# Making the one-hots, the shifted numbers and the transposed mask of a graph network on GpSimd, with a redrawn order of steps

## The chip, the core and the metric

The kernel runs on one core of a Trainium2 chip. A core has engines that work side by side, each through its own instructions in order: TensorE (PE; its weight loads are shown as PEld), VectorE (DVE), ScalarE (ACT), GpSimd (POOL) and SyncE (SP), which here issues nearly all the transfers between memories. They wait for each other through semaphores. Data stand in SBUF, on 128 partitions; TensorE writes its products to PSUM, which DVE and ACT can read and GpSimd can't. The metric is the time of one execution on the device, in microseconds (us).

## What is computed

A network of four layers over 128 graphs of 128 nodes with 64 features. Each layer normalises the features and adds its result to them. The first layer is the costly one, and the change lies in it:

```python
mask = (adj > 0.0).astype(x.dtype)
W1a, W1b = (W1[:F], W1[F:])
xj_proj = x @ W1a
diff = x[:, :, None, :] - x[:, None, :, :]
h = jax.nn.relu(xj_proj[:, :, None, :] + diff @ W1b + b1)
hm = jnp.einsum('bjkh,bjk->bjh', h, mask)
deg = jnp.sum(mask, axis=-1)
return hm @ W2 + deg[..., None] * b2
```

For every node j and every neighbour k of it (about an eighth of the nodes) a vector of H = 192 is formed, `relu(p[j] - q[k])`, and these are summed over the neighbours. Layer 1 is three matrix products with the adjacency and a head, layer 2 one product and a normalisation over the whole batch, layer 3 one product and a tanh.

## The kernel before

**Rounds.** The 128 graphs are worked on in 32 groups of G = 4. While one group is in the sum over neighbours, the next is sorted and projected, and the one before goes through layers 1 and 2. So in a steady state there is a round: the same mix of work on three neighbouring groups. Layer 3 follows at the end for all groups, after the sums over the batch.

**The sum over neighbours.** The kernel doesn't run over all 128 x 128 pairs. `sort` (line 535) numbers the neighbours of each node and sorts the nodes by how many they have. Step number n of a group then takes "the n-th neighbour of each node". A step has four parts, each a stream of its own:

- `pick` (709) makes the step's one-hot: a matrix with a 1 where the neighbour's number equals the wanted one. It is a comparison with a constant, from numbers in bf16 to 0 or 1 in bf16. Two sorts exist. `ohn` (128 x 1536, line 720) holds the one-hots of three steps at once, for near neighbours whose numbers come from `near_n`; there are NEAR = 4 in a group. `oh` (128 x 512, line 730) serves one step; there are FULL + BLOCKS = 5 + 3, five from `num` and three from `num_r`.
- `fill` (733) copies the sorted p, `psort` or `psort_r`, into one of three PSUM blocks `blk` (ACT).
- `subtract` (741) lets TensorE multiply the one-hot with q and add that into the block: q is gathered by a matrix product. A step with `oh` needs 12 products, as q is kept in three bf16 parts; a step with a third of `ohn` needs 4, from `near_q`.
- `gather` (756) takes the relu of the block and adds it to `acc` (DVE, `scalar_tensor_tensor` on 128 x 768).

A group has 20 steps. `ohn` has three buffers and `oh` five; `pick` may make the next one only when the step that used the buffer's last contents has been issued (lines 717 and 726).

**What stands around it.** In `sort`, ACT copies the transposed adjacency, `mT` (544) is its mask in bf16, TensorE counts with it (`ps_rankT`), DVE makes `leftT`, and so on to the sorting matrix `to_b`. GpSimd widens that to f32 (`to`, 593). The numbers `num` are copied out by ACT and sent through memory by SP (`n_dram`, then `near_n`, lines 609 to 611). `num_r` (627 to 636) are the numbers of the nodes with many neighbours, copied into segments and shifted by a constant for each segment: four `tensor_scalar` and one `tensor_tensor`. In `project` (639), GpSimd subtracts the third part of q (668), which SP then spreads into `near_q`, and adds the degree's share to x (675, 677). In `layer1` and `layer2_norm`, GpSimd makes four additions and products more. These eight instructions a round are GpSimd's whole work in the steady state.

**The order.** Within an engine the order of the program is the order of execution. It is made by `run_all` (1011): each stage of each group is a stream of steps, every step has a due time from a plan (`SORT_PLAN`, `PROJECT_PLAN`, ..., lines 49 to 55, with the groups PERIOD apart; `MOVED` and `OWN` for the first and last groups), and of the streams that may go on the one that is due first issues its next step. The plans are in units of 10 ns of a schedule that was worked out beforehand; on the chip they only set the order, the time comes from the engines and the waits.

All instructions are issued through one helper, so the profile puts them on its line 93; the tiles' names tell them apart.

Of the kernel before, what the change touches and what calls it, by code (L numbers as in the profile page):

```python
# [14 lines left out]
ALU = mybir.AluOpType  # L15
# [14 lines left out]
NEAR = 4  # L30
FULL = 5
BLOCKS = 3
SEGS = [76, 33, 11, 4, 2, 2]
STARTS = [sum(SEGS[:s]) for s in range(len(SEGS))]
# [10 lines left out]
MOVED = {('pick', -1): (49, 0.75), ('pick', -2): (-108, 1.095), ('fill', -1): (0, 0.75), ('fill', -2): (0, 1.0), ('subtract', -1): (-22, 0.752), ('subtract', -2): (21, 0.99), ('gather', -1): (0, 0.75), ('gather', -2): (20, 1.0), ('pick', 0): (-948, 0.849), ('fill', 0): (-93, 0.923), ('subtract', 0): (-63, 0.963), ('gather', 0): (-211, 0.71), ('sort', 0): (89, 0.76), ('sort', 1): (-572, 0.733), ('project', 0): (690, 0.648), ('project', 1): (-17, 1.008), ('after_layer0', 0): (0, 1.0)}  # L45
OWN = {('after_layer0', -2): [-663, 6, 139, 139, 387, 588, 694, 1072, 1098, 1186, 1287, 1312, 1312, 1472, 1598, 1676, 1789, 1789, 1972, 1972, 2122, 2482, 2482, 2482, 2482, 2717, 2869, 2913, 3118, 3160, 3171, 3319, 3423, 3497, 3650, 3650, 3804, 3804, 3839, 3858, 3896, 4188, 4290, 4321, 4633, 4697, 4724, 5099], ('first_half', -1): [-1189, -966, -886, -871, -753, -659, -570, -311, -230, -110, -107, -26, -26, 24, 49, 159, 231, 233, 351, 355, 454, 465, 465, 520, 582, 606, 717, 717, 879, 909, 909, 998, 1084, 1149, 1238, 1238, 1283, 1313, 1390, 1404, 1404, 1660, 1664, 1695, 1826, 1968, 1987, 2288], ('second_half', -1): [-1130, -987, -834, -770, -655, -586, -484, -231, -231, -153, -109, -52, -17, 45, 104, 176, 245, 247, 361, 365, 461, 472, 472, 525, 585, 608, 715, 745, 882, 913, 913, 1094, 1094, 1143, 1233, 1233, 1276, 1304, 1389, 1389, 1389, 1608, 1655, 1697, 1831, 1955, 1980, 2266], ('sort', 0): [-764, -520, -520, -118, 341, 397, 448, 545, 565, 586, 586, 586, 716, 719, 1143, 1143, 1539, 1889, 1889, 1889, 1889, 1889], ('project', 0): [-1552, -1066, -1066, -841, -472, 891, 1108, 2201, 3381, 3462, 3495, 3495, 3495, 3665, 3716, 3716, 3745, 3970, 3970, 3970, 3970, 4141, 4141, 4141, 4141, 4141, 4721, 5455, 5455]}
SET_UP_PLAN = [332, 1387, 1507, 1851, 1896, 1910, 1910, 2766]
PERIOD = 3491
SORT_PLAN = [-10, 215, 250, 378, 489, 489, 1032, 1058, 1156, 1168, 1185, 1185, 1446, 1511, 1511, 1575, 1776, 1776, 2087, 2287, 2309, 2309]
PROJECT_PLAN = [-2635, -2500, -1975, -1764, -1068, -475, 40, 1245, 1273, 1409, 1839, 1847, 1877, 2328, 2526, 2526, 2712, 2745, 2745, 2745, 2745, 2745, 2784, 3028, 3028, 3157, 3402, 3527, 3708]  # L50
PICK_PLAN = [-540, -447, -447, -276, -234, -22, 71, 77, 77, 77, 207, 1130, 1692, 2294]
FILL_PLAN = [-651, -523, -37, 207, 312, 687, 695, 888, 1110, 1226, 1432, 1432, 1606, 1644, 1929, 2176, 2386, 2562, 2724, 2886, 3026]
SUBTRACT_PLAN = [-1022, -1000, -991, -991, -991, -991, 205, 218, 476, 476, 699, 705, 715, 715, 715, 715, 936, 936, 936, 936, 984, 1048, 1230, 1504, 1504, 1511, 1760, 2121, 2121, 2305, 2305, 2419, 2419, 2783, 2851, 2851, 2902, 3090, 3152, 3168, 3252]
GATHER_PLAN = [-431, -241, 167, 444, 478, 731, 928, 1096, 1311, 1311, 1455, 1837, 2058, 2095, 2187, 2459, 2540, 2668, 2668, 2668, 3062]
AFTER_PLAN = [-636, -55, 123, 159, 454, 633, 843, 1365, 1400, 1517, 1608, 1727, 1799, 1930, 2098, 2203, 2347, 2353, 2590, 2597, 2796, 2819, 2819, 2929, 3055, 3102, 3327, 3385, 3651, 3713, 3728, 3925, 4064, 4163, 4337, 4337, 4423, 4476, 4618, 4644, 4655, 5082, 5218, 5260, 5500, 5761, 5797, 6329]
LATE = 14
WARM = 60
BEHIND = 3
# [50 lines left out]
def network(ctx, tc, io, out, over=None, x1=None):  # L109

    nc = Engines(tc)
# [42 lines left out]
    proj, near_q, near_n = [], [], []  # L154
# [175 lines left out]
    def set_up_first():  # L330

        yield
        nc.vector.tensor_scalar(wq, wp, -1.0, None, ALU.mult)
        nc.vector.tensor_tensor(wp, wp, wtop, ALU.add)
        done.add("w")
        yield
        centred(b2_all, F)
        yield from split_part(where["L0_gnn_b1"])
        for t in (near_q[1:] + near_n[1:]):
            nc.gpsimd.memset(t, 0.0)  # L340
        done.add("first")
        yield
# [76 lines left out]
    def flat(t):  # L419
        return t.rearrange("p a n -> p (a n)")  # L420
# [114 lines left out]
    def sort(g):  # L535
# [5 lines left out]
        adjT = adjTs[g]  # L541
        yield
        mT = once.tile([P, G, P], BF16, tag="mT", name="mT")
        nc.vector.tensor_scalar(mT, adjT, 0.0, None, ALU.is_gt)
        yield BANK
        pk = bank("ps_rankT")
        matmul(pk, upto_t, flat(mT), start=True, stop=True)
# [58 lines left out]
        num = edge.tile([P, G, P], BF16, tag="num", name="num")  # L606
# [19 lines left out]
        yield  # L626
        num_r = edge.tile([P, G, P], BF16, tag="num_r", name="num_r")
        for i in range(LIKE):
            nc.vector.tensor_scalar(num_r[:, :, STARTS[i] : STARTS[i] + SEGS[i]], num[:, :, 0 : SEGS[i]], float(-i * BLOCKS), None, ALU.add)
        m, n = len(SEGS) - LIKE, SEGS[LIKE]  # L630
        nc.vector.tensor_tensor(
            num_r[:, :, STARTS[LIKE] : P].rearrange("p b (m n) -> p b m n", n=n),
            num[:, :, 0:n].unsqueeze(2).to_broadcast([P, G, m, n]),
            behind.unsqueeze(1).unsqueeze(3).to_broadcast([P, G, m, n]),
# [74 lines left out]
    def pick(g):  # L709

        yield lambda: g in sorts
        for n, (third, i) in enumerate(ORDERS.get(g, ORDER)):
            t = g * per + n
            if third is not None:
                if (g, i) not in nears:
                    k = len(nears)
                    yield lambda: k < 3 or near_last[k - 3] in ready
                    near_last.append(max(g * per + m for m, kind in enumerate(ORDERS.get(g, ORDER)) if kind[0] is not None and kind[1] == i))
                    oh = nears[g, i] = ohn.tile([P, 3, G, P], BF16, tag="ohn", name="ohn")
                    nc.vector.tensor_scalar(oh.rearrange("p t b n -> p (t b n)"), near_n[g % 2].rearrange("p t b n -> p (t b n)"), float(i + 1), None, ALU.is_equal)  # L720
                    onehots[t] = oh[:, third]
                else:
                    onehots[t] = nears[g, i][:, third]
                continue
            k = len(other_last)
            yield lambda: k < 5 or other_last[k - 5] in ready
            other_last.append(t)
            num = sorts[g][0 if i < FULL else 1]
            oh = ohp.tile([P, G, P], BF16, tag="oh", name="oh")
            nc.vector.tensor_scalar(flat(oh), flat(num), float(NEAR + i + 1), None, ALU.is_equal)  # L730
            onehots[t] = oh

    def fill(g):
# [285 lines left out]
    if x1 is not None:  # L1019
        run(set_up_first())  # L1020
        run(set_up())
        for g in range(NG - 1):
            run(after_layer0(g))
    else:
        streams = []
        early = -9 * PERIOD
        streams.append(Stream(set_up_first(), SET_UP_PLAN, early))
        streams.append(Stream(set_up(), REST_PLAN, 0))
        for g in range(NG):
            for stage, plan, start in (  # L1030
                (sort, SORT_PLAN, (g - 1) * PERIOD if g else early),
                (project, PROJECT_PLAN, (g - 1) * PERIOD if g else early),
                (pick, PICK_PLAN, g * PERIOD),
                (fill, FILL_PLAN, g * PERIOD),
                (subtract, SUBTRACT_PLAN, g * PERIOD),
                (gather, GATHER_PLAN, g * PERIOD),
                *(((after_layer0, AFTER_PLAN, (g + 1) * PERIOD),) if g < NG - SPLIT else ((first_half, AFTER_PLAN, (g + 1) * PERIOD), (second_half, AFTER_PLAN, (g + 1) * PERIOD))),
            ):
                key = stage.__name__, g if g < 2 else g - NG
                later, scale = MOVED.get(key, (0, 1.0))  # L1040
                streams.append(Stream(stage(g), OWN.get(key, plan), start + later, scale))
        streams.append(Stream(squares(), SQUARES_PLAN, (NG - 1) * PERIOD))
        streams.append(Stream(filler(), FILLER_PLAN, (NG - 1) * PERIOD))
        run_all(streams)
# [319 lines left out]
```

## Time and profile before

| | us |
|---|---|
| runs of the kernel before: median (lowest to highest) | 1360.82 (1359.75 to 1364.78) |
| the profiled execution | 1361.02 |
| its span, first to last instruction | 1359.0 |
| mean clock granted to TensorE in it | 0.98 |
| busy: ACT | 974.6 (72%) |
| busy: GpSimd | 327.7 (24%), 408 instructions |
| first and last `oh` on DVE start at | 25.0 and 1183.7 |

After the last step of the last group there follow about 165 us of batch sums and layer 3.

How to read it: the profile lists for each engine when each instruction was at work. Its groups of instructions are written "engine operation out<-in shapes xcount | busy us, mean ns of one | idle time of the engine just before them, and what ended it". The chain of waits follows the work that ended last back from the end, at each step to what released it; "issue" is time in which the engine waited for nothing that shows. A line of busy time by engine has the stretch, its length, then PE, PEld, DVE, ACT and POOL, each with the number of instructions, the granted clock, the share of the transfer engines that was in use and GB/s.

GpSimd's larger instructions in the steady state, by their mean: the subtraction for q 1651 ns, the addition to the adjacency 1286, the widening of `to` 766, the others 615 to 761. In the 1359 us it stood idle for 308.7 us until ACT had made q, 291.2 us until DVE had made t, and 234.2 us until DVE had made `to_b`.

### The profile page before, as it was taken

What the parts mean: (1) busy time and instruction counts of PE and PEld (TensorE: products, weight loads), DVE (VectorE), ACT (ScalarE), POOL (GpSimd) and SP (SyncE); (2) the same over time, 40 slices, a digit from 0 to 9 for tenths busy, and PEclk for the clock granted to TensorE, in tenths of its full rate; (3) what the DMA queues carried; (4) which work ended last, traced back from release to release, by engine and by line L of the source; (5) the groups of instructions that cost most, each with busy time, mean ns of one, the idle gap of its engine ahead of it and who ended that gap; (6) DMA issues with size and microseconds to landing.
All of it is one profiled execution on the core that took longest, in us unless ns stands there. A gap on an engine that the chain in (4) does not pass through costs nothing.

```text
span 1359.0 us, 29824 instructions
## 1 busy us (share of the span) xinstructions
PE 1195.3 (88%) x11031; PEld 983.3 (72%) x11031; DVE 1138.3 (84%) x2573; ACT 974.6 (72%) x1871; POOL 327.7 (24%) x408
## 2 busy tenths in 40 slices
PE   5689999999999999998989999999999988889787
PEld 2467777777777777777777777777777777777566
DVE  6888988888888888888888888888888888735894
ACT  3577777777788777777777777777877777743653
POOL 3421122211221112221112221221211222012983
PEclk9899999999999999999999999999999999986899
DMA  2222222222222122222222222222222221100254
GB/s 81 78 70 68 67 70 61 68 73 72 72 73 73 53 70 65 67 67 67 70 66 65 68 69 73 72 72 72 63 62 64 65 63 58 40 9 9 78 153 116
DMA packets 106997, 92.41 MB, mean 68 GB/s; under 512 B 45135, under 2 KB 90460, under 8 KB 106844
## 3 DMA queue, kind: packets, MB, share of 16 engines
q1 hardware_dynamic: 106380, 90.17, 23.1%
q8 instruction: 89, 1.46, 0.5%
q14 instruction: 64, 0.52, 0.1%
q10 hardware_dynamic: 464, 0.26, 0.1%
HBM read 34.12 MB, written 16.71 MB: 37 GB/s over the span
## 4 chain that ended last, share of the span: by engine, by line
DVE 45%; PE 40%; issue 6%; POOL 3%; ACT 3%; SPq 1%; DVEq 1%; DMA 0%; ACTq 0%; POOLq 0%
DVE acc L93 24%; PE blk L93 17%; PE ps_pr L93 5%; PE ps_ag L93 4%; PE ps_sA L93 4%; PE ps_p L93 4%; DVE x L93 2%; PE ps_q L93 2%; DVE h L93 2%; PE ps_ga L93 2%; DVE lower L93 2%; SPq L93 1%; DVE rank L93 1%; DVE rank_t L93 1%; DVE to_b L93 1%
## 5 line engine op out<-in xcount | busy, mean ns | idle before, releaser
L93 DVE SCALAR_TENSOR_TENSOR acc<-blk,acc 128x768 f32<-128x768 f32 x576 | 545.3, 951 | 102.3 <-PE blk L93 68.7
L93 ACT COPY blk<-psort 128x768 f32<-128x768 f32 x544 | 428.2, 803 | 43.4 <-DVE acc L93 42.1
L93 PE MATMUL blk<-q,oh 128*128 128x192 bf16 x3072 | 302.5, 247 | 46.9 <-ACT blk L93 43.6
L93 PEld LDWEIGHTS <-oh 128*128 128x128 bf16 x3072 | 260.9, 99 | 81.2 <-issue 72.8
L93 PE MATMUL blk<-near_q,ohn 128*128 128x192 bf16 x1536 | 183.8, 246 | 18.6 <-ACT blk L93 16.1
L93 PEld LDWEIGHTS <-ohn 128*128 128x128 bf16 x1536 | 134.1, 99 | 61.5 <-issue 49.9
L93 POOL TENSOR_TENSOR q<-rest,q 128x768 bf16<-128x768 f32 x32 | 52.8, 1651 | 308.7 <-ACT q L93 308.6
L93 POOL TENSOR_TENSOR x<-x,t 128x260 f32<-128x260 f32 (+1 forms) x33 | 24.0, 729 | 291.2 <-DVE t L93 291.2
L93 ACT COPY blk<-psort_r 128x768 f32<-128x768 f32 x96 | 78.6, 818 | 16.3 <-DVE acc L93 16.0
L93 PEld LDWEIGHTS ps_pr<-g,dT 128*128 128x128 f32 x504 | 71.3, 192 | 20.4 <-issue 7.0
L93 POOL CAST to<-to_b 128x512 f32<-128x512 bf16 x32 | 24.5, 766 | 234.2 <-DVE to_b L93 234.2
L93 DVE TENSOR_SCALAR ohn<-near_n 128x1536 bf16<-128x1536 bf16 x128 | 80.5, 630 | 0.0
L93 PE MATMUL ps_pr<-g,dT 128*128 128x128 f32 x504 | 78.6, 279 | 0.6 <-ACT dT L93 0.5
L93 PE MATMUL ps_ag<-adjT,msg 128*128 128x128 f32 x504 | 68.8, 279 | 0.0
L93 ACT ACTIVATE dT<-ps_ag 128x512 f32<-128x512 f32 (+1 forms) x96 | 57.6, 600 | 7.1 <-PE ps_ag L93 4.9
L93 ACT ACTIVATE rstd<-var,eps 128x4 f32<-128x4 f32 (+1 forms) x98 | 29.4, 300 | 45.4 <-DVE var L93 45.4
L93 PEld LDWEIGHTS ps_ag<-adjT,msg 128*128 128x128 f32 x504 | 61.5, 192 | 0.2 <-ACT sB L93 0.2
L93 ACT COPY psort<-ps_p 128x384 f32<-128x384 f32 x64 | 30.7, 479 | 41.8 <-PE ps_p L93 41.8
L93 PE MATMUL ps_q<-wq,hT 128*128 128x384 f32 x128 | 59.1, 546 | 0.8 <-ACT hT L93 0.5
L93 PE MATMUL ps_sA<-fro,acc 128*128 128x128 f32 x248 | 50.2, 284 | 9.2 <-DVE acc L93 8.6
L93 ACT ACTIVATE sq<-x 128x256 f32<-128x256 f32 (+1 forms) x98 | 39.7, 407 | 19.4 <-DVE x L93 19.4
L93 PE MATMUL ps_p<-wp,hs 128*128 128x384 f32 x128 | 53.0, 496 | 0.6 <-ACT hs L93 0.5
(272 smaller groups left out, 2595.9 us busy)
## 6 DMA issues: line engine op xcount, KB each, us to landing
near_q<-q SPq DMA_DIRECT2D x288, 63.0 KB
near_n<-n_dram SPq DMA_DIRECT2D x96, 126.0 KB
a<-in_adj_dram SPq DMA_DIRECT2D x32, 256.0 KB
adjT_dram<-adjT SPq DMA_DIRECT2D x32, 256.0 KB
adjT<-adjT_dram SPq DMA_DIRECT2D x32, 256.0 KB
psort_r<-psort SPq DMA_DIRECT2D x32, 228.0 KB
fro_r<-fro SPq DMA_DIRECT2D x32, 152.0 KB
x<-in_x_dram SPq DMA_DIRECT2D x32, 128.0 KB
```

The costliest lines, as they stand in the source:

```text
L93: ins = op(*args, **kw)
```

## The change

The comparisons for `ohn` and `oh`, the transposed mask `mT` and the five instructions for `num_r` are issued on GpSimd instead of DVE. Their operands, buffers and gates stay. `PERIOD` and the seven plans of the steady state are new numbers; `MOVED`, `OWN`, the set-up plans and the plans of the end are unchanged. Of the plans, those for projecting and picking are shown; sorting, filling, subtracting, gathering and the layers after are redrawn in the same manner.

```diff
-PERIOD = 3491
+PERIOD = 3436
...
-PROJECT_PLAN = [-2635, -2500, -1975, -1764, -1068, -475, 40, 1245, 1273, 1409, 1839, 1847, 1877, 2328, 2526, 2526, 2712, 2745, 2745, 2745, 2745, 2745, 2784, 3028, 3028, 3157, 3402, 3527, 3708]
-PICK_PLAN = [-540, -447, -447, -276, -234, -22, 71, 77, 77, 77, 207, 1130, 1692, 2294]
...
+PROJECT_PLAN = [-3200, -3200, -3200, -3200, -3200, -3185, -760, 1256, 1345, 1387, 1651, 1745, 1821, 2240, 2315, 2369, 2429, 2706, 2706, 2706, 2706, 2706, 2726, 2849, 2865, 3006, 3033, 3096, 3274]
+PICK_PLAN = [-1036, -1030, -995, -995, -995, -995, -660, -575, 579, 642, 700, 1003, 1228, 1228]
...
         mT = once.tile([P, G, P], BF16, tag="mT", name="mT")
-        nc.vector.tensor_scalar(mT, adjT, 0.0, None, ALU.is_gt)
+        nc.gpsimd.tensor_scalar(mT, adjT, 0.0, None, ALU.is_gt)
...
         for i in range(LIKE):
-            nc.vector.tensor_scalar(num_r[:, :, STARTS[i] : STARTS[i] + SEGS[i]], num[:, :, 0 : SEGS[i]], float(-i * BLOCKS), None, ALU.add)
+            nc.gpsimd.tensor_scalar(num_r[:, :, STARTS[i] : STARTS[i] + SEGS[i]], num[:, :, 0 : SEGS[i]], float(-i * BLOCKS), None, ALU.add)
         m, n = len(SEGS) - LIKE, SEGS[LIKE]
-        nc.vector.tensor_tensor(
+        nc.gpsimd.tensor_tensor(
...
-                    nc.vector.tensor_scalar(oh.rearrange("p t b n -> p (t b n)"), near_n[g % 2].rearrange("p t b n -> p (t b n)"), float(i + 1), None, ALU.is_equal)
+                    nc.gpsimd.tensor_scalar(oh.rearrange("p t b n -> p (t b n)"), near_n[g % 2].rearrange("p t b n -> p (t b n)"), float(i + 1), None, ALU.is_equal)
...
-            nc.vector.tensor_scalar(flat(oh), flat(num), float(NEAR + i + 1), None, ALU.is_equal)
+            nc.gpsimd.tensor_scalar(flat(oh), flat(num), float(NEAR + i + 1), None, ALU.is_equal)
```

More of the change, by code (lines that the diff above doesn't have):

```diff
@@ L47 @@
 SET_UP_PLAN = [332, 1387, 1507, 1851, 1896, 1910, 1910, 2766]
-PERIOD = 3491
-SORT_PLAN = [-10, 215, 250, 378, 489, 489, 1032, 1058, 1156, 1168, 1185, 1185, 1446, 1511, 1511, 1575, 1776, 1776, 2087, 2287, 2309, 2309]
-PROJECT_PLAN = [-2635, -2500, -1975, -1764, -1068, -475, 40, 1245, 1273, 1409, 1839, 1847, 1877, 2328, 2526, 2526, 2712, 2745, 2745, 2745, 2745, 2745, 2784, 3028, 3028, 3157, 3402, 3527, 3708]
-PICK_PLAN = [-540, -447, -447, -276, -234, -22, 71, 77, 77, 77, 207, 1130, 1692, 2294]
@@ L52 @@
-FILL_PLAN = [-651, -523, -37, 207, 312, 687, 695, 888, 1110, 1226, 1432, 1432, 1606, 1644, 1929, 2176, 2386, 2562, 2724, 2886, 3026]
-SUBTRACT_PLAN = [-1022, -1000, -991, -991, -991, -991, 205, 218, 476, 476, 699, 705, 715, 715, 715, 715, 936, 936, 936, 936, 984, 1048, 1230, 1504, 1504, 1511, 1760, 2121, 2121, 2305, 2305, 2419, 2419, 2783, 2851, 2851, 2902, 3090, 3152, 3168, 3252]
-GATHER_PLAN = [-431, -241, 167, 444, 478, 731, 928, 1096, 1311, 1311, 1455, 1837, 2058, 2095, 2187, 2459, 2540, 2668, 2668, 2668, 3062]
@@ L55 @@
-AFTER_PLAN = [-636, -55, 123, 159, 454, 633, 843, 1365, 1400, 1517, 1608, 1727, 1799, 1930, 2098, 2203, 2347, 2353, 2590, 2597, 2796, 2819, 2819, 2929, 3055, 3102, 3327, 3385, 3651, 3713, 3728, 3925, 4064, 4163, 4337, 4337, 4423, 4476, 4618, 4644, 4655, 5082, 5218, 5260, 5500, 5761, 5797, 6329]
+PERIOD = 3436
+SORT_PLAN = [-278, -118, 153, 213, 532, 576, 794, 939, 1049, 1101, 1142, 1174, 1391, 1449, 1554, 1557, 1734, 1821, 1853, 2115, 2131, 2212]
+PROJECT_PLAN = [-3200, -3200, -3200, -3200, -3200, -3185, -760, 1256, 1345, 1387, 1651, 1745, 1821, 2240, 2315, 2369, 2429, 2706, 2706, 2706, 2706, 2706, 2726, 2849, 2865, 3006, 3033, 3096, 3274]
@@ new lines @@
+PICK_PLAN = [-1036, -1030, -995, -995, -995, -995, -660, -575, 579, 642, 700, 1003, 1228, 1228]
+FILL_PLAN = [-187, -115, 75, 75, 238, 311, 489, 547, 840, 874, 940, 1153, 1354, 1361, 1857, 2013, 2254, 2427, 2594, 2594, 2803]
+SUBTRACT_PLAN = [-54, -54, 8, 8, 8, 8, 433, 433, 433, 457, 457, 619, 691, 901, 932, 932, 932, 964, 999, 1102, 1158, 1264, 1264, 1513, 1545, 1594, 1702, 1888, 1950, 2040, 2040, 2040, 2040, 2040, 2409, 2837, 2837, 2837, 2837, 2929, 2929]
+GATHER_PLAN = [111, 111, 238, 347, 449, 650, 742, 907, 1089, 1280, 1280, 1622, 1859, 1910, 2060, 2485, 2485, 2485, 2608, 2758, 2763]
@@ L56 @@
+AFTER_PLAN = [-139, -116, -88, 53, 282, 642, 689, 1281, 1488, 1524, 1610, 1703, 1703, 1838, 2006, 2034, 2179, 2284, 2284, 2517, 2517, 2517, 2709, 2895, 2922, 2961, 3074, 3089, 3177, 3534, 3744, 3885, 3925, 3925, 4066, 4151, 4225, 4284, 4362, 4384, 4432, 5019, 5122, 5230, 5372, 5485, 5648, 5823]
 LATE = 14
```

## The prediction

> **What bounds the kernel now.** I read first the busy times of the page, then the whole-span chain of waits, then the busy time per engine in one group's round, then that round's own chain. The first line is the page's; the next two are pieces of the whole-span chain (start, duration, what); then one round's busy time by engine; the last five are pieces of the chain inside that round.
>
> ```profile
> PE 1195.3 (88%) x11031; PEld 983.3 (72%) x11031; DVE 1138.3 (84%) x2573; ACT 974.6 (72%) x1871; POOL 327.7 (24%) x408
> ...
> 794.93 2.02 PE ps_sA L93 x16
> 831.19 2.02 PE ps_sA L93 x16
> ...
> 797.80:834.10 36.30, 33.11 (x313) 27.58 (x311) 31.93 (x68) 28.28 (x54) 6.88 (x8) 1.00 0.23 67
> ...
> 799.88 0.20 DVE oh L93
> 800.08 0.34 DVE mT L93
> 807.83 0.47 DVE ohn L93
> 815.19 0.20 DVE oh L93
> 830.04 0.06 DVE oh L93
> ```
>
> The same piece returns after 831.19 - 794.93 = 36.26 us: that is one round, the work on one group of four graphs. In a round of 36.30 us TensorE is busy 33.11 us, DVE 31.93, ACT 28.28, GpSimd 6.88. So no engine alone fills the round. Over its first 20 us the chain runs almost wholly on DVE, after that on TensorE. DVE's one-hots and mT hold 0.20 + 0.34 + 0.47 + 0.20 + 0.06 = 1.27 us of the chain; GpSimd has 29.4 us free in the round.
>
> **What is removed.** These are the rows of the costliest groups on DVE, over 32 rounds: busy time, then mean ns of one.
>
> ```profile
> L93 DVE TENSOR_SCALAR ohn<-near_n 128x1536 bf16<-128x1536 bf16 x128 | 80.5, 630 | 0.0
> L93 DVE TENSOR_SCALAR oh<-num 128x512 bf16<-128x512 bf16 x160 | 45.4, 303 | 0.0
> L93 DVE TENSOR_SCALAR oh<-num_r 128x512 bf16<-128x512 bf16 x96 | 27.2, 283 | 0.6 <-PE blk L93 0.6
> L93 DVE TENSOR_SCALAR mT<-adjT 128x512 bf16<-128x512 f32 x32 | 13.5, 420 | 3.4 <-ACT adjT L93 3.4
> L93 DVE TENSOR_SCALAR num_r<-num 128x304 bf16<-128x304 bf16 x32 | 8.3, 258 | 0.0
> ```
>
> Per round: 4 x 0.630 + 5 x 0.303 + 3 x 0.283 + 0.420 = 5.30 us, and five small ones for num_r of 258, 193, 173, 163 and 166 ns (0.95 us). DVE falls from 31.9 to about 25.7 us. Of that only the 1.27 us above stands in the chain; the rest is hidden, half under TensorE's stretch, half in DVE's slack.
>
> **What is added.** The same 18 instructions on GpSimd, which the trace of before does not show at this size. The rows below are GpSimd's own, from the set-up at 51 to 67 us: the same operation and types on 3 partitions, and the cheapest one-input operation it has.
>
> ```profile
> L93 POOL TENSOR_SCALAR c<-c,ident 3x449 bf16<-3x449 bf16 x2 | 2.8, 1412 | 0.2
> L93 POOL CAST c<-cat 3x449 bf16<-3x449 f32 x3 | 1.7, 555 | 8.0 <-DVE cat L93 7.8
> L93 POOL TENSOR_SCALAR c<-c,ident 3x128 bf16<-3x128 bf16 x2 | 1.2, 598 | 0.2
> L93 POOL CAST c<-cat 3x128 bf16<-3x128 f32 x3 | 0.8, 282 | 0.2
> L93 POOL TENSOR_TENSOR q<-rest,q 128x768 bf16<-128x768 f32 x32 | 52.8, 1651 | 308.7 <-ACT q L93 308.6
> ```
>
> TENSOR_SCALAR: (1412 - 598) / (449 - 128) = 2.54 ns an element, 273 ns fixed. CAST: (555 - 282) / 321 = 0.85 ns, 173 ns fixed. That 3 partitions may stand for 128 is seen at TENSOR_TENSOR: its rows on 3 partitions (f32, 1030 and 418 ns at 449 and 128) give 1.91 ns and 174 ns fixed, so 1.64 us at 768 elements; the 128-partition row has 1.651 us.
>
> By the TENSOR_SCALAR line: ohn (1536) 4.17 us, four of them 16.7; oh (512) 1.57 us, eight of them 12.6; mT 1.57; num_r (304, 132, 44, 16 elements and a TENSOR_TENSOR of 0.2) 2.55. Sum 33.4 us, with the 6.9 us there now 40.3 us: more than the round of 36.26. GpSimd becomes the bound. By the CAST line: 1.48, 0.61, 0.61 and 1.31 us give 12.7 us, with 6.9 together 19.6 us: it fits easily. A third line, steeper, through the 604 ns of the other 3x128 TENSOR_SCALAR row and the 222 ns of a 1-element one (3.01 ns an element), gives 37.8 + 6.9 = 44.7 us. GpSimd just fills 36.26 us at about 2.2 ns an element (29.4 us free, less 18 x 0.26 fixed = 24.7, over 11,248 elements). I take 2.54: same engine, same operation, same types; what differs is the compare and a constant instead of a per-partition scalar, and nothing in the trace says that these make it three times cheaper.
>
> The Trainium skill, page GPSIMD Engine Reference, section 4.1 Engine selection, says the opposite: only two-input operations are slow there, one-input ones run at roughly line rate. At the 1.03 cycles an element of its section 3.1 and 1.2 GHz that is 0.86 ns (an estimate from the page), and GpSimd would need about 21 us, no bound at all. The CAST row agrees with the page, the TENSOR_SCALAR row doesn't, being three times that.
>
> **The port the two engines share.** DVE's x<-mean,per_f handles 4 elements and has two SBUF inputs:
>
> ```profile
> L93 DVE TENSOR_TENSOR x<-mean,per_f x32: 157/570/998, 7.5 to 1105.5; 128x4 f32<-128x4 f32 x32
> ...
> 813.50 0.74 POOL L93 CAST to<-to_b 128x512 f32<-128x512 bf16 x1 [6.77 <-DVE to_b L93]
> 813.69 0.57 DVE L93 TENSOR_TENSOR x<-mean,per_f 128x4 f32<-128x4 f32 x1
> ```
>
> It takes 157 ns alone and 570 where it starts inside GpSimd's CAST: it ends when the CAST does. In the other direction the y<-y,nrm of GpSimd took 1.03 us instead of 0.62 where a DVE ohn had started at its side. So each holds the other up for what is left of the one begun first. Seven DVE instructions of a round have two SBUF inputs (h x3 at 0.43, the second rank 0.68, x<-mean,x 0.42, x<-mean,per_f 0.16, counted 0.16: 2.7 us). Each can now wait for the rest of a GpSimd one-hot: by the durations above 1.2 us on average (sum of squares 101 over twice 40.3), some 8.7 us a round. That takes DVE to 34.4 us, still hidden under GpSimd's 40.3. Back the other way, GpSimd loses between 0 and 2.7 us a round; I take 1.35. What the changed order removes of such meetings: DVE's own ohn and oh, which met GpSimd, are gone from DVE.
>
> The Trainium skill, page SBUF — State Buffer, section Who interferes with whom, has this as an exclusive lock that is kept for a whole instruction. If it holds at 4 us too, a single DVE operation could stand 4.2 us; no row here is that long.
>
> **The sum.** A round of 40.3 + 1.35 = 41.65 us against 36.26: 5.4 us more. 31 rounds pay (in the first the other engines still wait for the first loads): 167 us. The plan's new order can't give it back, as the sum of one engine's work does not depend on order. DVE's 1.27 us in the chain bring nothing then. 1359.0 us of span + 167 + the 2.0 us around the span (1361.02 for the profiled execution, 0.2 above the median of 1360.82) = 1528; I say 1525. With no loss at the port it is 1359 + 31 x 4.0 + 2 = 1485, with all of it 1569, with the steeper line and 1.35 us 1665.
>
> **Waits and queues.** GpSimd works in order and issues no DMA here. Behind its one-hots now stand `to` (PE ps_ga waits), q's last third (the third of three near_q transfers on SP waits; behind that on SP psort_r and the next group's loads), x + t, x + db, the adjT add and y times nrm: each now starts up to 4.2 us late. mT goes from 0.42 to 1.57 us ahead of ps_rankT and leftT, num_r from 0.95 to 2.55 ahead of three one-hots. A one-hot's buffer (5 of oh, 3 of ohn) frees only when TensorE has used it, so a waiting ohn also holds up these. All that is hidden as long as GpSimd itself is the bound; where it isn't, it is the third case below. The new due times (picks by 5 to 11 us earlier, centre and norm of the next group earlier) move instructions but add none; near_n's transfers on SP keep their place behind num. I cost the reordering at 0: TensorE's 33.1 us cover it, and without that cover it is worth at most the 1.27 us a round.
>
> **Rivals.**
> 1. Faster: the compare runs near CAST's 0.85 ns. GpSimd then has 19.6 us of 36. Gain: 1.27 us in the chain, less 0.27 for mT (0.61 for 0.34), less half of the port's waits on DVE (seven, each 0.54 of the time busy, 0.5 us mean rest: 1.9, half on DVE's stretch 0.9), at least nothing and at most 1.0 us; I take half, 0.55 x 31 = 17 us: 1344, from 1328 to 1354. For: the CAST rows. Against: the TENSOR_SCALAR rows, six of them alike. It decides below about 1.5 ns an element.
> 2. Slower, but not by GpSimd's sum: 1.5 to 2.2 ns, GpSimd 80 to 100% busy. One-hots come just in time, seven DVE instructions wait some 0.9 us each (6 us, as much as was taken off DVE), and `to`, q and x + t each stand behind an ohn of 2.6 to 3.6 us. At half to one us a round in the chain: 1361 + 15 to 31 = 1376 to 1392.
> 3. No change: the gain on DVE and its waits at the port cancel, 1354 to 1368.
>
> **Chances.** GpSimd as the bound 0.60, rival 2 0.12, no change 0.06, rival 1 0.22. Slower by over 0.5% (which is about what a measurement of this kernel tells from no change) 0.72, same 0.06, faster 0.22. The likeliest case by itself: 1440 to 1640. The range over the cases, 1340 to 1620, leaves out the better half of rival 1 and the steeper line, some 0.18.
>
> **What will show it.** GpSimd's ohn rows at 4.2 us and oh at 1.6 (right), or 1.5 and 0.6 (rival 1); GpSimd over 95% busy in a round, 0.7 of the chain its own; ps_sA returning after 41 to 42 us; TensorE's idle time ending on GpSimd's oh and ohn; DVE's h and rank lengthened to over 1 us. The prediction is wrong if a compare costs under 2.2 ns an element, or if GpSimd stands idle waiting for DVE's t or to_b while it is the slowest.

## The result, and the profile after

The changed kernel takes 1636.87 us (median of 4 runs, 1633.14 to 1640.22) against 1361.12 us before (median of 4): a ratio of 1.202, 95% interval 1.1984 to 1.2056. Forecast were 1525 us, with a range of 1340 to 1620. The direction and the engine were right, the size was 112 us short.

The page of the changed kernel: busy times, the chain's shares by engine, and the one-hots (busy us, mean ns | idle before them, and what ended it).

```profile
PE 1263.5 (77%) x11031; PEld 1067.5 (65%) x11031; DVE 1055.0 (64%) x1997; ACT 993.9 (61%) x1871; POOL 1340.4 (82%) x984
...
POOL 35%; DVE 25%; PE 22%; issue 9%; ACT 5%; DMA 2%; SPq 1%; DVEq 0%; POOLq 0%; ACTq 0%
...
L93 POOL TENSOR_SCALAR ohn<-near_n 128x1536 bf16<-128x1536 bf16 x128 | 523.4, 4089 | 19.1 <-DMA near_n<-n_dram 11.2
L93 POOL TENSOR_SCALAR oh<-num 128x512 bf16<-128x512 bf16 x160 | 238.0, 1487 | 12.3
```

GpSimd is the busiest engine now, and an ohn costs 4.09 us there instead of 0.63 on DVE. But it is not busy all the time: it holds only 35% of the chain. One round in a line of busy time by engine (stretch, length, PE, PEld, DVE, ACT, POOL, clock):

```profile
1031.90:1075.80 43.90, 34.78 (x311) 29.94 (x311) 29.48 (x50) 28.85 (x54) 38.64 (x27) 0.93 0.19 56
```

A round takes 44 us, and GpSimd is at work for 38.6 of it. Over 18 steady rounds of its timeline I summed what lies between: 1.22 us a round are pauses of under 0.2 us from one instruction to the next, 4.29 us are real waits. The timelines of the engines at the end of one round and the start of the next show where these come from (start, us, engine, instruction [idle before, releaser]):

```profile
1058.60 4.10 POOL L93 TENSOR_SCALAR ohn<-near_n 128x1536 bf16<-128x1536 bf16 x1
1062.78 3.05 POOL L93 TENSOR_SCALAR oh<-num 128x512 bf16<-128x512 bf16 x2
1065.89 4.08 POOL L93 TENSOR_SCALAR ohn<-near_n 128x1536 bf16<-128x1536 bf16 x1
1069.94 1.64 POOL L93 TENSOR_TENSOR q<-rest,q 128x768 bf16<-128x768 f32 x1
...
1059.19 0.83 ACT L93 CAST q<-rest 128x768 bf16<-128x768 f32 x1
...
1061.37 12.61 SPq L93 DMA_DIRECT2D near_q<-q  x9
...
1071.61 0.80 ACT L93 ACTIVATE extra<-psort,spare_n 128x192 f32<-128x192 f32 x2 [4.29 <-POOL q L93]
...
1072.94 0.80 PE L93 MATMUL ps_sA<-fro,acc 128*128 128x128 f32 x2 [4.81 <-ACT dT L93]
...
1075.76 0.96 DVE L93 SCALAR_TENSOR_TENSOR acc<-blk,extra 128x768 f32<-128x768 f32 x1 [8.72 <-ACT blk L93]
...
1037.73 0.73 POOL L93 TENSOR_TENSOR x<-x,t 128x260 f32<-128x260 f32 x1 [3.79 <-DVE t L93]
...
1081.85 0.73 POOL L93 TENSOR_TENSOR x<-x,t 128x260 f32<-128x260 f32 x1 [4.03 <-DVE t L93]
```

ACT has written the second part of q by 1060.0, but GpSimd's subtraction for the third part stands behind an ohn, two oh and another ohn and starts at 1069.94, 9.9 us later. Until it is done ACT stands 4.3 us, TensorE 4.8 us, DVE 8.7 us, and SP can't send the last three near_q transfers. Then all of them work off what was held up. A few us into each round (here at 1037.73 and 1081.85) GpSimd itself waits 3.8 to 4.0 us for DVE's t, the result of layer 1 for the group one before. t isn't computed from the late q. It is late because its product stands behind the first sum's products on TensorE, and t itself behind the first sum on DVE. The busiest engine waits for work that it delayed itself.

The round is this ring: from x + t at 1037.73 to the end of q at 1071.58 GpSimd works for 33.9 us with no pause above 0.1 us, and from there it takes 10.3 us until t is there and the next x + t starts at 1081.85. Together that is 44.1 us.

The plans themselves put q there, and the change shows it. In the new plans the first four one-hots of the next group are due at -995 + 3436 = 2441, and q's step at 2706. In the old plans q's step was due at 2745, ahead of the first one-hot at -447 + 3491 = 3044.

### The profile page after: what moved, and what is told of

It reads as the page before. It is cut to its first block, busy times and chain, and to the rows that moved or that the text cites. A ratio compares the mean times of both kernels' runs of the same rounds, so it can differ in the third digit from the quotient of the medians.

```text
span 1637.8 us, 29872 instructions
## 1 busy us (share of the span) xinstructions
PE 1263.5 (77%) x11031; PEld 1067.5 (65%) x11031; DVE 1055.0 (64%) x1997; ACT 993.9 (61%) x1871; POOL 1340.4 (82%) x984
## 4 chain that ended last, share of the span: by engine, by line
POOL 35%; DVE 25%; PE 22%; issue 9%; ACT 5%; DMA 2%; SPq 1%; DVEq 0%; POOLq 0%; ACTq 0%
POOL ohn L93 16%; DVE acc L93 13%; PE blk L93 10%; POOL oh L93 9%; PE ps_sA L93 6%; DVE h L93 3%; POOL q L93 3%; PE ps_pr L93 2%; DVE rank L93 2%; POOL num_r L93 2%; ACT extra L93 2%; POOL y L93 1%; DMA near_n<-n_dram 1%; ACT blk L93 1%; ACT dT L93 1%
## 5 line engine op out<-in xcount | busy, mean ns | idle before, releaser
L93 POOL TENSOR_SCALAR ohn<-near_n 128x1536 bf16<-128x1536 bf16 x128 | 523.4, 4089 | 19.1 <-DMA near_n<-n_dram 11.2
L93 PE MATMUL blk<-near_q,ohn 128*128 128x192 bf16 x1536 | 223.4, 259 | 58.0 <-ACT blk L93 57.7
L93 POOL TENSOR_SCALAR oh<-num 128x512 bf16<-128x512 bf16 x160 | 238.0, 1487 | 12.3
L93 PEld LDWEIGHTS ps_sA<-fro,acc 128*128 128x128 f32 x248 | 64.9, 321 | 157.3 <-ACT dT L93 156.6
L93 POOL TENSOR_SCALAR oh<-num_r 128x512 bf16<-128x512 bf16 x96 | 142.8, 1487 | 7.6
L93 ACT ACTIVATE extra<-psort,spare_n 128x192 f32<-128x192 f32 x128 | 50.6, 445 | 153.1 <-POOL q L93 153.1
L93 DVE SCALAR_TENSOR_TENSOR h<-x,rstd 128x256 f32<-128x256 f32 (+1 forms) x98 | 84.4, 861 | 14.8 <-PE ps_ga L93 9.6
L93 PE MATMUL ps_sA<-fro_r,acc 128*128 128x128 f32 x248 | 76.3, 410 | 0.0
L93 DVE TENSOR_TENSOR rest<-ps_q,q 128x384 f32<-128x384 f32 x64 | 35.3, 552 | 56.6 <-ACT q L93 56.6
L93 POOL TENSOR_SCALAR num_r<-num 128x304 bf16<-128x304 bf16 (+3 forms) x128 | 66.0, 524 | 5.6 <-ACT num L93 1.5
```

The source lines that it names most:

```text
L93: ins = op(*args, **kw)
```

## The experiments

The first four ask which of the change's parts costs what, and whether the wait for q is the cause. All times are us; "round" is the mean distance of the first sum of a group over 18 steady rounds, worked out from the trace. Where no interval is given, it is one run; the kernel before took 1358 to 1366 beside them.

**e1_own_extra: `extra` no longer shares a buffer with `rest`.** ACT waits before `extra` because its buffer is the one that q's subtraction still reads.

```diff
-        extra = once.tile([P, NP, W], F32, tag="rest", name="extra")
+        extra = once.tile([P, NP, W], F32, tag="extra", name="extra")
```

> The changed kernel, with one difference: the tile extra gets a buffer of its own instead of the one it shares with rest (room is made by two buffers instead of three for the loaded adjacency). Theory: a round is 44.15 us although GpSimd is busy only 38.6 us of it, because ACT may not write extra before GpSimd's subtraction for q has read rest, and that subtraction stands in GpSimd's queue behind two ohn and two oh; ACT, TensorE and DVE stand still until then, t comes late, and GpSimd then waits 3.8 us for t. With a buffer of its own ACT no longer waits for q; the near_q transfers still do. Round 40 to 42 us, span 1490 to 1560 us, ACT's idle time before extra near 0 (was 153 us), GpSimd's wait for t under 60 us (was 129). Rival, the shared port (DVE's h and rank held up by one-hots make t late): nothing changes, 1620 to 1645. Rival, near_q's last third is what everything waits for: 1600 to 1640, with TensorE's wait for ACT dT gone and a wait for the near_q transfer of the same length in its place.

1637.63: nothing is gained. The waits, by engine and releaser (us, times, longest):

```profile
DVE acc L93 <- PE blk L93: 353.9, 131, 21.9
...
POOL x L93 <- DVE t L93: 132.6, 31, 11.2
PE blk L93 <- issue: 80.6, 15, 18.8
PE blk L93 <- DMA near_q<-q: 74.7, 15, 8.3
```

ACT's wait for q is gone, and TensorE waits before its products with near_q in its place: 15 times for the transfer of q by name, 74.7 us, and 15 times, 80.6 us, with no releaser that the profile shows. The shared buffer was a second wait of the same length behind the same instruction. The third reading in the expectation was the right one by its waits (its time is also that of the second), my theory's detail was wrong. It leaves two candidates for the root: q's place in the queue, or the port.

**e2_q_on_dve: q's subtraction on DVE.**

```diff
-        nc.gpsimd.tensor_tensor(parts_q[:, 2], rest, parts_q[:, 1], ALU.subtract)
+        nc.vector.tensor_tensor(parts_q[:, 2], rest, parts_q[:, 1], ALU.subtract)
```

> The changed kernel, with q's third part subtracted on DVE instead of GpSimd. Theory (what stands still in a round stands still for q behind the one-hots): q is there about 9 us earlier, both extra and near_q's last third with it; GpSimd has 38.6 - 1.6 = 37.0 us of work in a round and little to wait for: round 37 to 39 us, span 1400 to 1465 us. Rival, the shared port: only the 1.64 us are gained, round 42.5 us, span about 1585. Rival, GpSimd's order as such (one-hots that wait for their buffers): 1570 to 1600.

1488.44, round 39.26. 148 us are gained for an instruction of 1.64 us (51 us over 31 rounds); the time is 23 us above what the theory allowed. Now GpSimd is what the forecast had taken it for, in the page's chain and in one round:

```profile
POOL 59%; DVE 17%; PE 11%; issue 6%; DMA 4%; ACT 2%; SPq 1%; DVEq 0%; POOLq 0%; ACTq 0%
...
901.00:940.16 39.16, 32.67 (x312) 27.58 (x311) 31.07 (x51) 28.84 (x54) 37.65 (x26) 1.00 0.22 63
```

37.7 us of work, 1.3 of short pauses and 0.2 of waiting are the round. It is 0.7 us more work than 38.6 - 1.6; 0.5 of it is a pair of oh that takes 3.58 instead of 3.05 us beside DVE's new subtraction.

**e3_plan_alone and e4_old_plan: order and engine apart.** e3 is the kernel before with the new PERIOD and the seven new plans; e4 is the change with the old ones (the diffs are the lines of the change shown above, each half by itself).

> The kernel before with the new plans and PERIOD, all one-hots, mT and num_r on DVE. Whether the redrawn order by itself costs or gains. Theory (the order is worth at most what DVE has in the chain, 1.27 us a round): 1340 to 1385 us, near 1362. Rival, the redrawn order is the cost: over 1450.

> The change with the plans of the kernel before: one-hots, mT and num_r on GpSimd, picks due 5 to 11 us later than in the changed kernel. GpSimd's work in a round stays 38.6 us. Theory (GpSimd's sum plus what it waits for because its order puts q behind one-hots): GpSimd is ahead by less, so more waits: 1640 to 1760 us. Rival, the new order is to blame for the idle 5.5 us a round: 1450 to 1560.

| | old plans | new plans |
|---|---|---|
| on DVE | 1361 | 1485 (e3; ratio 1.089, 1.0859 to 1.0921) |
| on GpSimd | 1844 (e4) | 1637 (the change) |

In e3 the theory was wrong and the rival's time, over 1450, came: the new order costs 124 us by itself, a round of 40.0 us. With the work on GpSimd it gains 207. Moving the work costs 482 us under the old order, more than both ranges for e4 allowed, and 152 under the new. So the two halves don't add, and neither can be read as a share of the whole. What e3's order does to the steps is seen where the instructions on the PSUM blocks waited, first before, then e3 (us, times):

```profile
  PE blk L93: 141.9, 113
  ACT blk L93: 62.2, 104
  DVE acc L93: 60.2, 103
```

```profile
  PE blk L93: 178.2, 83
  DVE acc L93: 165.9, 272
  ACT blk L93: 148.9, 251
```

Waits for ACT's copies (104 before, 251 in e3) and for DVE's sums (103, 272) are about two and a half times as frequent, while waits for TensorE's products are fewer (113, 83) but longer. Which of the seven plans does that was not separated.

In e4 the waits were, first of all:

```profile
ACT sB L93 <- PE ps_sB L93: 463.6, 32, 16.4
PE ps_rankT L93 <- POOL mT L93: 444.3, 32, 16.8
```

GpSimd's timeline there has q ahead of the one-hots, and mT behind them (one round; six more one-hots lie between these lines):

```profile
906.43 1.64 POOL L93 TENSOR_TENSOR q<-rest,q 128x768 bf16<-128x768 f32 x1 [4.00 <-ACT q L93]
...
910.01 4.10 POOL L93 TENSOR_SCALAR ohn<-near_n 128x1536 bf16<-128x1536 bf16 x1
...
928.70 1.49 POOL L93 TENSOR_SCALAR oh<-num 128x512 bf16<-128x512 bf16 x1
930.27 1.49 POOL L93 TENSOR_SCALAR oh<-num_r 128x512 bf16<-128x512 bf16 x1
931.83 1.49 POOL L93 TENSOR_SCALAR mT<-adjT 128x512 bf16<-128x512 f32 x1
```

So mT is what comes late, and TensorE's queue stands behind ps_rankT, 14 us a round.

**e6_q_earlier: the change with one due time moved.** The most direct test of the place in the queue, with the work on each engine as it was. The new due time is ahead of the four one-hots due at 2441:

```diff
-PROJECT_PLAN = [..., 2315, 2369, 2429, 2706, 2706, ...]
+PROJECT_PLAN = [..., 2315, 2369, 2429, 2430, 2706, ...]
```

> The changed kernel with one due time changed: the step of project that issues q's last subtraction on GpSimd and its near_q transfers comes at 2430 instead of 2706, so ahead of some of the one-hots that stood before it. GpSimd's work stays 38.6 us a round. Theory (what is lost beyond GpSimd's sum is lost because q stands behind one-hots, and near_q with it): round 39.5 to 42 us, span 1495 to 1560. Rival (GpSimd's 1.64 us for q and the port, not its place in the queue): 1610 to 1640.

1565.75, round 41.47: 71 us for one number (6 above the range). GpSimd's timeline:

```profile
917.71 1.65 POOL L93 TENSOR_TENSOR q<-rest,q 128x768 bf16<-128x768 f32 x1 [1.53 <-ACT q L93]
919.33 4.10 POOL L93 TENSOR_SCALAR ohn<-near_n 128x1536 bf16<-128x1536 bf16 x1
923.51 3.06 POOL L93 TENSOR_SCALAR oh<-num 128x512 bf16<-128x512 bf16 x2
```

q goes first, and GpSimd now waits 1.5 us for ACT instead of 3.9 for t: 38.66 + 1.28 + 1.54 = 41.48, the round. Of GpSimd's 4.29 us of waits a round 1.54 are left, so q's place in the queue is shown as the cause of most of them. The port isn't what made them: in e6 DVE's h is held up longer than in the change (a mean of 1357 ns against 876), and the round is 2.7 us shorter all the same.

**e7_old_plan_mt_on_dve: is it one late instruction, then?** e4 with mT on DVE.

```diff
-        nc.gpsimd.tensor_scalar(mT, adjT, 0.0, None, ALU.is_gt)
+        nc.vector.tensor_scalar(mT, adjT, 0.0, None, ALU.is_gt)
```

> The change under the plans of the kernel before (51.0 us a round, GpSimd busy 38.6 of it), with mT back on DVE. Theory: there TensorE's queue stands some 14 us a round on ps_rankT, which waits for mT, which stands behind one-hots; without that a round falls to GpSimd's 37.2 us and a little, at most to 42: span 1420 to 1580. Rival (another late instruction of GpSimd takes its place at once): 48 to 51 us a round, 1750 to 1840.

1727.51, round 48.0: a miss for the theory; the round is the rival's, the time 22 us below its range. 116 us are gained, then other waits take over: ACT's queue waits for GpSimd's x (244 us in all), and GpSimd for to_b (3.6 us a round, 2.2 in e4) and still for ACT's q (4.0, as in e4). Under this order mT is not the only instruction of GpSimd that comes late for someone.

**e8_num_r_alone and e9_num_r_oh_r: a smaller dose,** old plans, num_r alone, then num_r and its three oh on GpSimd.

```diff
-            nc.vector.tensor_scalar(flat(oh), flat(num), float(NEAR + i + 1), None, ALU.is_equal)
+            (nc.vector if i < FULL else nc.gpsimd).tensor_scalar(flat(oh), flat(num), float(NEAR + i + 1), None, ALU.is_equal)
```

> The kernel before with num_r alone on GpSimd, old plans. GpSimd gets 2.3 us more a round, DVE 0.95 us less. No num_r stands in the chain of before. Theory (a small part of the work that meets no queue is free and brings next to nothing): 1352 to 1370. Rival (any longer work on GpSimd costs through the port or its queue): 1372 to 1400.

> The kernel before with num_r and the three oh of num_r on GpSimd, old plans. GpSimd at 6.9 + 2.3 + 4.5 = 13.7 us a round, DVE 1.8 us less. Theory (the old plan makes these one-hots only just ahead of their use, so 1.49 us instead of 0.28 shows where DVE was not late): 1358 to 1390. Rival (DVE's relief wins): 1330 to 1350. Rival (a wait in GpSimd's queue for x + t or to_b holds the one-hots up): over 1400.

1363.94, ratio 1.0022 (1.0012 to 1.0032), and 1366.09, ratio 1.0037 (1.0022 to 1.0052). Both lie in the range of their theory. With GpSimd at 9.2 and 14.1 us a round it is far from full, and still nothing is won: a round stays at 36.27 and 36.45. What was to be won at all?

**e10_few_onehots_before and e11_few_onehots_after: 9 of 12 comparisons left out,** in the kernel before and in the changed one.

```diff
                 if third is not None:
+                i = 0
...
+            if i not in (0, FULL):
+                onehots[t] = oh_of[g, i >= FULL]
+                continue
```

> The kernel before, where only the first ohn and the first oh of each sort are made in a group and the other steps use these again (9 of 12 comparisons are left out): DVE does 3 x 0.55 + 6 x 0.28 = about 3.7 us less in a round (3 of 4 ohn, 6 of 8 oh), nothing goes to GpSimd. It measures what the move could have won at most on DVE's side. Theory (one-hots and mT hold 1.27 us of a round's chain, mT stays): 0.5 to 1 us a round, 1325 to 1348. Rival (DVE's work bounds the round): 3 us a round, 1260 to 1300. Rival (other paths are as long): over 1350.

> The changed kernel with the same 9 of 12 comparisons left out: GpSimd's work in a round falls from 38.6 to 38.6 - 3 x 4.09 - 6 x 1.49 = 17.5 us, order and engines as in the change. Theory (the time went to GpSimd's sum and to what stood behind it): the round falls below 40 us, to what the new plan gives by itself: 1400 to 1490. Rival (the longer way over GpSimd and the port at each meeting, whatever its sum): over 1550.

e10: 1342.95, ratio 0.9855 (0.9838 to 0.9871), round 35.56. The nine comparisons are 3.7 us by their own times, and DVE's busy time falls by 2.6 us a round (31.9 to 29.3). Giving them to no one is worth 0.7 us a round, 20 us in all, as the theory had it. Moving these nine could hardly have brought more under the old order; leaving out the other three, mT and num_r as well was not run. e11: 1389.55, round 36.20, 10 us below its range. With GpSimd at 17.8 us the same order and the same engines are back at the old round: the 247 us between the change and e11 hang on these nine comparisons. Fewer one-hots also mean fewer waits for their buffers, in both runs; that was not separated.

**e5_ohn_on_dve and e12_q_mt_on_dve: where GpSimd stops being the bound,** both under the new plans: ohn back on DVE; q and mT on DVE.

> The changed kernel with the four ohn of a round back on DVE: GpSimd at 38.6 - 16.4 = 22.3 us a round, DVE 2.2 us more than in the changed kernel, new plan. Theory: GpSimd no longer bounds, no instruction of it stands behind 4 us ones; what is left is the new plan, which took 1485 us with everything on DVE: 1420 to 1490. Rival (any queueing on GpSimd is the cost, the eight oh are enough): over 1530.

> The changed kernel with q's last subtraction and mT on DVE (one step beyond the run with q alone on DVE, which had a round of 39.15 us and 1488 us). If with q gone GpSimd's sum is the round, taking another 1.49 us from GpSimd shortens the round by the same 1.5 us: 37.7 us, 1435 to 1450. Rival (something else, the plan or TensorE, has already taken over): 38.8 to 39.2 us, 1475 to 1490.

e5: 1446.68, as its theory had it, round 38.48 with GpSimd at 23.2 us. e12: 1467.95, between its two ranges, round 38.74 with GpSimd at 36.3 + 1.25 of pauses, and GpSimd waits 1.1 us for t. Taking 1.49 us from e2's GpSimd gained 0.5 us a round, not 1.5: in e12 the chain is DVE 38%, PE 32%, ACT 18%, GpSimd 4%. So at about 38.5 us a round something else than GpSimd has taken over. What it is wasn't separated; e3, with all of it on DVE, is near it at 40.0.

The rounds side by side:

| run | us | round | GpSimd busy | short pauses | its waits |
|---|---|---|---|---|---|
| before | 1361 | 36.29 | 6.9 | 0.1 | - |
| after | 1637 | 44.14 | 38.6 | 1.2 | 4.3 |
| e1 own buffer for extra | 1638 | 44.11 | 38.6 | 1.3 | 4.2 |
| e6 q earlier | 1566 | 41.47 | 38.7 | 1.3 | 1.5 |
| e2 q on DVE | 1488 | 39.26 | 37.7 | 1.3 | 0.2 |
| e12 q, mT on DVE | 1468 | 38.74 | 36.3 | 1.3 | 1.2 |
| e4 old plans | 1844 | 51.04 | 39.2 | 1.2 | 10.6 |
| e7 old plans, mT on DVE | 1728 | 47.98 | 37.8 | 1.3 | 8.9 |

## Why the prediction was right, and where it was wrong

**The price of a comparison: right.** Forecast were 2.54 ns an element and 273 ns fixed, from four small TENSOR_SCALAR instructions on 3 partitions. The rows after give (4089 - 1487) / 1024 = 2.54 ns and 186 ns fixed. The 18 moved instructions take 32.1 us a round (33.4 forecast), all of GpSimd's 38.6 (40.3). The Trainium skill (GPSIMD Engine Reference, section 4.1 Engine selection) calls one-input operations roughly line-rate. That does not hold for this operation: 2.54 ns is three times the 0.86 ns that the prediction worked out, as an estimate, from the page's section 3.1. Rival 1 fell with it; the 20 us that e10 gained are near the 17 at which it was priced, but no run here has a cheap comparison on GpSimd.

**What DVE's relief is worth: right in size.** 1.27 us a round stood in the chain; e10 found 0.7 us for nine of the twelve comparisons.

**The port: right in kind, too large.** Of DVE's seven instructions h and the second rank were held up: h has a mean of 876 ns against 429 before, rank 1453 against 679. x<-mean,per_f, which the CAST had held up before, is free of it (158 ns against 558). That is 3 x 0.45 + 0.77 - 0.40 = 1.7 us a round more on DVE, not 8.7, and DVE has slack: it is busy for 29.5 us of a round. GpSimd's side was costed at 1.35 us a round; its ohn rows run from 4079 to 4111 ns and its oh rows from 1486 to 1560, so its one-hots lost next to nothing. That DVE's side isn't what makes the round is seen in e6; no run takes the port's waits away by themselves.

**The failed step is this one: "All that is hidden as long as GpSimd itself is the bound".** I had listed q's subtraction, near_q, x + t and mT as up to 4.2 us late and costed them at nothing, because a full engine can't be waited for twice. But GpSimd also waits for what stands behind its late results in the other engines' queues: q, then extra and near_q, TensorE's products, DVE's first sum, t, and GpSimd's x + t. It waits 4.3 us a round, 3.9 of them at the end of that ring. And q is not 4.2 but 9.9 us late, since four one-hots stand ahead of it. The prediction had read the new due times as "picks by 5 to 11 us earlier" (three of the fourteen are 5 to 6 us later) and had not set them against q's own. Its last sentence had named the sign: GpSimd "stands idle waiting for DVE's t or to_b while it is the slowest". GpSimd is busy for 87% of a round, where over 95% was expected, and holds 0.35 of the chain instead of 0.7. e6 takes most of these waits away by moving q ahead of the one-hots, e2 by taking q off GpSimd; e1 shows that near_q waits behind the same q, so that freeing the buffer that ACT waited for gains nothing.

**A second step was wrong with it:** "I cost the reordering at 0", and at most the 1.27 us a round. e3 measures 3.7 us a round for the order without the move. In the change it doesn't add: there the new order is better than the old by 207 us.

The sum in the trace's terms, of 278.8 us more span: 31 rounds x (38.63 - 36.29) = 73 for GpSimd's work beyond the old round, 31 x 1.22 = 38 for its short pauses, which I had left out, and 31 x 4.29 = 133 for its waits (the slower clock below is in them); 17 until the first sum (50.7 us against 33.7); 13 after the last; the 5 that remain lie in the uneven first and last rounds. Forecast were 125 for the work, 42 for the port and nothing for the rest.

## What to carry to other kernels

Before work goes to an idle engine, price it by that engine's own rows of the same operation, and add what the engine does already: here 32 + 7 us against a round of 36 settled the sign. Then look at the short instructions that are on it already. Each can now stand behind the long ones; compare their due times with those of the new work. If others' queues stand for such an instruction, and the engine itself waits further down for them, the delay costs time even though the engine is the bound; one due time was worth 71 us. And ask first what the relief can bring: leaving nine of the twelve comparisons out altogether gained 20 us.

## What was not expected of the hardware

**TensorE's clock falls in every round.** After the 4.8 us in which it waits for q, the granted clock is halved (stretch, length, PE, PEld, DVE, ACT, POOL, clock):

```profile
1060.00:1068.00 8.00, 8.00 (x73) 6.93 (x71) 5.23 (x8) 5.07 (x10) 7.78 (x4) 1.00 0.21 61
1068.00:1072.90 4.90, 0.12 (x2) 0.00 (x0) 0.00 (x0) 1.29 (x4) 4.82 (x4) 0.91 0.00 0
1072.90:1077.20 4.30, 4.26 (x20) 4.12 (x21) 1.40 (x3) 3.35 (x6) 3.91 (x4) 0.50 0.30 79
```

Twenty products take 4.3 us there; the sixteen of ps_sA had taken 2.02 us in a piece of the chain before, and a ps_sA product has a mean of 438 ns against 284. So the wait makes the products after it, and t with them, later still; how much of the round that is was not measured. The Trainium skill (TensorE: Matmul & The Clock Gate, Part 1) names a window of about 3.4 us without work after which the clock halves. The 4.8 us here agree, and the waits of before, none above 0.9 us in the steady rounds, left it at 1.00. But e3 shows that less can be enough: its clock halves in about half of its steady rounds, though TensorE waits there for 1.7 us at most. One of these stretches, with the one before it:

```profile
720.00:728.90 8.90, 5.80 (x65) 4.54 (x66) 8.36 (x15) 6.44 (x12) 2.17 (x3) 1.00 0.26 77
728.90:732.30 3.40, 3.40 (x27) 2.94 (x24) 2.64 (x6) 1.91 (x3) 0.41 (x1) 0.50 0.00 0
```

**A held-up DVE instruction goes on before GpSimd's ends.** Timeline of the changed kernel:

```profile
1041.35 1.82 DVE L93 SCALAR_TENSOR_TENSOR h<-x,rstd 128x256 f32<-128x256 f32 x1
...
1039.67 4.09 POOL L93 TENSOR_SCALAR ohn<-near_n 128x1536 bf16<-128x1536 bf16 x1
```

h needs 0.43 us, so it was at work from about 1042.74, 1.0 us before the row of ohn ends at 1043.76. The rule of the Trainium skill (SBUF — State Buffer, section Who interferes with whom), a lock for the whole instruction, would have let it start only then. The rows of GpSimd overlap each other a little (the ohn of 1065.89 ends at 1069.97, q starts at 1069.94), so their ends aren't exact; this is a difference in the record, not a proof.
